# Four graph layers on one core: list keys and layer 0's row operations on other engines, and PSUM banks shared out anew

## The chip, the cores and the metric

The kernel runs on one core of one Trainium2 chip. The metric is the device time of one execution in microseconds (us); the time of the kernel before is the median of three runs. A core has five engines, which run side by side, each through its own list of instructions in a fixed order: TensorE (PE, matrix products), VectorE (DVE), ScalarE (ACT), GpSimd (POOL) and SyncE (SP, which issues most DMA transfers). An engine that has to wait holds up everything that stands behind in its list. SBUF is the on-chip memory that all of them use, and PSUM, eight banks of 128 x 512 numbers of 32 bits, is where TensorE writes. VectorE and ScalarE also read and write PSUM. GpSimd does not.

## The reference, cut to what matters

Eight batches of 2048 nodes with 64 features pass through four graph layers with one adjacency matrix. The matrix is sparse (some rows have over a hundred neighbours, most have a few), and each layer takes a softmax over a node's neighbours.

```python
# layer 0
h = jnp.maximum(_layernorm(x), 0.0)
x = x + attention(h, h, mask=adj)            # scores h.h / 8, values h
# layer 1
h = jnp.maximum(_layernorm(x), 0.0) @ W1
x = x + elu(softmax(leaky(h@a1 [:,None] + h@a2 [None,:]), adj) @ h)
# layer 2: four heads of dot-product attention with W_h, then W_o, one more attention, layer norm
# layer 3: as layer 1 with relu for elu
```

## The kernel before, in words

All eight batches are processed together: a row tile is 128 nodes by 512 numbers (8 batches x 64 features), and there are 16 row tiles, called i. A table in DRAM holds one row of 512 or 520 numbers for every node. A node's neighbours are fetched from it by indirect DMA, issued by GpSimd, one slot of 128 rows at a time (`gather`, L253). Each tile has a number of slots K for its nodes' first neighbours (`ROWS`, L29) and T packed slots for the neighbours left over (`PACKED`, L30). There are 81 slots in all. They land in a ring of 26 slots (`RING`, L33), so 26 gathers can be under way before the first slot has to be free again.

`edge_stack` (L62) writes the whole program. Inside, `pipeline` (L219) lays stages over the 16 tiles: in turn n, the last stage treats the oldest tile and the first stage the newest. A scheduler then arranges each engine's instructions. Within each layer the stages overlap, but between layers nothing does: a layer's gathers need every row of the table that the layer before wrote, the row of means among them (the neighbour of a node without any).

Five stretches follow each other.

- Stretch A (L711) normalises the 16 input tiles into table 0: row sums on VectorE (`norm_a`, L277), eight squares with a bias on ScalarE (L291), the sum of squares (L297), and eight scalings with relu on ScalarE (L308). `store_rows` (L362) stores the tile and adds it into `acc` on GpSimd (L367, L369). At the last tile, one product with `ones` makes the mean row (L372).
- Layer 0 (L712) builds each tile's neighbour lists and uses them. `load_adj` (L618) loads 128 x 2048 integers. `lists` (L622) turns each positive entry into a key, its column number counted from the right, in one VectorE operation (L627). VectorE's `max` then takes the eight largest keys of each segment (L633, `segments` L48, `SEGS` L32), with `match_replace` where more are wanted (L635), and again over the segments' results (L643, L645); small operations make the indices (L653, L708), masks (L655, L709) and selection matrices (L680). `take0` gathers; `first0` computes scores on VectorE (L432 to L441); `second` (L471) weights the gathered rows on GpSimd (L390) and sums them on TensorE (L395). `third0` (L483) divides on VectorE (L481), adds to x (L489), and normalises again (`norm_a` with `centre`: mean L281, subtraction L284, both on VectorE). `pre_c` scales on ScalarE, and table 1 is stored.
- Layer 1 (`additive`, L516) takes its scores from two numbers for each node, weights its rows on VectorE (L390 again), and projects on TensorE (L571). `products` (L331) prepares layer 2.
- Layer 2 (L725 to L860), the longest, weights on GpSimd and scores on VectorE.
- Layer 3 comes in two parts: the second attention of the reference's layer 2 (L863 to L912, weights on GpSimd) and the last additive layer (L920, weights on VectorE).

A helper called `tiny` (L231) hands out columns of one PSUM bank, as a place for small operands that VectorE then reads from PSUM: the mean in `norm_a` (L280), the node's own numbers and the weights in `additive` (L541, L556), and the squared norms in `first3` (L880). The bank is the only one in pool `ps_t`. The other pools in layers 0, 1 and 3 are `ps_q` with 3 banks, and `ps_m` and `ps_y` with 2 banks each.

The constants and weights are loaded at the very start (L143 to L205), ahead of the first input tile on SP.

## Time and profile before

| | us |
|---|---|
| median of 3 runs | 1628.55 (1625.19 to 1629.81) |
| the profiled execution | 1627.04 |
| its span, first to last instruction | 1625.3 |
| VectorE busy | 1289.1 (79%) |
| TensorE busy | 1209.7 (74%) |
| GpSimd busy | 1015.0 (62%) |
| ScalarE busy | 771.0 (47%) |

A group of instructions stands in the profile as its line, engine, operation, output<-inputs, shapes and count, then its busy time and the mean length of one in ns, and then how long the engine had idled before it and what ended that. The stretches can be told by their gathers: the first gather of layer 0 is issued at about 108 us, that of layer 1 at 399, of layer 2 at 610, of layer 3's first part at 1175 and of its second part at 1462. An engine's busy time over the whole span says little here, since each stretch has its own limit; the busy times by stretch are read in the prediction.

### The profile page before, as it was taken

The numbers are of one execution on the slowest core, as the hardware profiler recorded it, in microseconds if no ns is written. First come the engines' busy times: TensorE is split into PE (matmuls) and PEld (weight loads), VectorE is DVE, ScalarE is ACT, GpSimd is POOL, SyncE is SP. The second block draws the span as 40 slices with busy tenths as digits, with TensorE's granted clock in tenths as the row PEclk, the third lists the DMA queues.
The fourth block names the chain that finished last, engine by engine and source line by source line (L and its number), as shares of the span: only waits on it lengthen the run. The fifth ranks groups of instructions, "written<-read, shape, count | busy, mean of one in ns | idle before, by whom it ended". The sixth has DMA issues, their size and how long they took to land. (4 is left out here: it accounts for less than half of the span.)

```text
span 1625.3 us, 15664 instructions
## 1 busy us (share of the span) xinstructions
PE 1209.7 (74%) x3771; PEld 607.8 (37%) x3771; DVE 1289.1 (79%) x2594; ACT 771.0 (47%) x2522; POOL 1015.0 (62%) x823
## 2 busy tenths in 40 slices
PE   0024766876799983699987999999766878855997
PEld 0012243444454531234343344443333334423555
DVE  6978999994689996899999699871159979954677
ACT  5861323444377882456532455555426446760011
POOL 4345865664763006898689889898276686527550
PEclk9999787787899997799999999999967987857899
DMA  5545555453787448566265344400084453227771
GB/s 177 179 152 190 179 189 174 142 186 122 225 289 264 155 160 309 203 207 211 66 223 185 121 151 170 164 13 7 30 313 139 125 168 120 79 79 218 214 211 61
DMA packets 85786, 266.93 MB, mean 164 GB/s; under 512 B 14627, under 2 KB 14659, under 8 KB 75446
## 3 DMA queue, kind: packets, MB, share of 16 engines
q0 software_dynamic: 37328, 141.05, 28.0%
q1 hardware_dynamic: 48358, 124.79, 21.8%
q8 instruction: 32, 0.52, 0.1%
q14 instruction: 68, 0.56, 0.1%
HBM read 208.74 MB, written 57.05 MB: 164 GB/s over the span
## 5 line engine op out<-in xcount | busy, mean ns | idle before, releaser
L260 POOL DMA_INDIRECT g<-table,idx x405 | 396.3, 978 | 234.2 <-issue 135.2
L783 POOL TENSOR_TENSOR wh<-g,w 128x1024 f32<-128x1024 f32 x162 | 307.3, 1918 | 35.6 <-PE y L798 33.6
L395 PE MATMUL y<-wg,ident 128*128 128x512 f32 x392 | 240.9, 744 | 50.2 <-POOL wg L390 44.2
L390 POOL TENSOR_TENSOR wg<-g,w 128x1024 f32<-128x1024 f32 (+1 forms) x91 | 155.1, 1717 | 74.8 <-ACT w L446 44.6
L770 DVE TENSOR_REDUCE s<-prod 128x32 f32<-128x2048 f32 x81 | 183.8, 2285 | 20.3 <-ACT w L772 19.9
L798 PE MATMUL y<-wh,ident 128*128 128x512 f32 x320 | 155.7, 614 | 22.7 <-POOL wh L796 20.6
L395 PE MATMUL y<-wg,selt 128*128 128x512 f32 x256 | 138.6, 651 | 8.7 <-POOL wg L390 8.1
L395 PEld LDWEIGHTS y<-wg,ident 128*128 128x128 f32 x392 | 83.2, 232 | 136.3 <-issue 67.4
L798 PE MATMUL y<-wh,selt 128*128 128x512 f32 x256 | 125.1, 614 | 12.1 <-POOL wh L783 12.1
L806 ACT ACTIVATE yn<-y,rec 128x64 f32<-128x64 f32 x512 | 111.3, 367 | 30.4 <-PE y L798 29.7
L369 POOL TENSOR_TENSOR acc<-acc,xh 128x512 f32<-128x512 f32 x45 | 58.0, 1288 | 96.8 <-ACT xh L308 84.6
L766 DVE TENSOR_TENSOR prod<-q,g 128x2048 f32<-128x2048 f32 x49 | 111.4, 2274 | 3.6 <-ACT g L764 3.3
L390 DVE TENSOR_TENSOR wg<-g,tiny 128x1024 f32<-128x1024 f32 (+1 forms) x92 | 98.2, 1085 | 11.6 <-PE y L395 11.2
L452 DVE SCALAR_TENSOR_TENSOR zt<-m,bhc,att 128x512 f32<-128x512 f32 x64 | 47.1, 736 | 75.3 <-ACT att L451 75.3
L438 PE MATMUL q<-rows,sel 128*128 128x512 f32 x128 | 84.3, 762 | 17.6 <-DVE prod L440 9.2
L798 PEld LDWEIGHTS y<-wh,ident 128*128 128x128 f32 x320 | 59.6, 195 | 96.9 <-issue 62.6
L409 PEld LDWEIGHTS m<-w,selt 128*128 128x128 f32 x384 | 62.6, 211 | 88.4 <-issue 26.2
L308 ACT ACTIVATE xh<-x,ln_r 128x64 f32<-128x64 f32 x256 | 88.3, 428 | 14.6 <-POOL ln_r L302 13.6
L409 PE MATMUL m<-w,selt 128*128 128x8 f32 (+1 forms) x384 | 59.7, 258 | 44.9 <-ACT w L555 17.2
L764 ACT COPY g<-g 128x512 f32<-128x512 f32 x81 | 50.4, 622 | 86.5 <-DVE prod L766 77.4
L790 PE MATMUL y<-rows,ident 128*128 128x512 f32 x128 | 70.2, 634 | 18.7 <-DVE prod L766 13.6
L766 DVE TENSOR_TENSOR prod<-qe,g 128x2048 f32<-128x2048 f32 x32 | 72.9, 2279 | 12.9 <-DMA qe<-qtab,qidx 11.7
(208 smaller groups left out, 2515.9 us busy)
## 6 DMA issues: line engine op xcount, KB each, us to landing
qtab<-q SPq DMA_DIRECT2D x16, 1040.0 KB, 4.3
a<-in_adj_dram SPq DMA_DIRECT2D x16, 1024.0 KB, 7.0
q<-qtab SPq DMA_DIRECT2D x14, 1040.0 KB, 6.3
table<-xh SPq DMA_DIRECT2D x48, 256.0 KB, 2.2
rows<-table SPq DMA_DIRECT2D x48, 256.0 KB, 3.6
xs<-x SPq DMA_DIRECT2D x48, 256.0 KB, 2.4
x<-xs SPq DMA_DIRECT2D x48, 256.0 KB, 4.6
table<-xh SPq DMA_DIRECT2D x32, 260.0 KB, 2.0
```

Source lines behind the costliest of these rows:

```text
L260: g = nc.gpsimd.indirect_dma_start(out=ring[:, (held[i] + t) % RING, :cols], out_offset=None, in_=table[k][:, :], in_offset=bass.IndirectO ...
L308: nc.scalar.activation(dst[:, b * D:(b + 1) * D], st["src"][:, b * D:(b + 1) * D], func, bias=0.0 if st["less"] is None else r[:, 1, b:b + ...
L390: eng.tensor_tensor(wg[:, :m].rearrange("p t (b d) -> p t b d", b=B), g[:, :, :F].rearrange("p t (b d) -> p t b d", b=B), w[:, t0:t0 + m, ...
L395: nc.tensor.matmul(y, lhs(i, t), wg[:, t - t0, :], start=(t == 0 and own is None), stop=(t == n - 1))
L409: nc.tensor.matmul(p[:, :cols], selt(i, t), packed[:, t, :], start=(t == 0), stop=(t == T - 1))
L438: nc.tensor.matmul(qe, sel(i, t - K), q, start=True, stop=True)
L766: nc.vector.tensor_tensor(pr.rearrange("p (b h) d -> p b h d", h=H), q[:, :B * H * D].rearrange("p (b h d) -> p b h d", h=H, d=D), heads(g ...
L770: nc.vector.tensor_reduce(s[:, t - lo, :], pr, AX.X, OP.add)
L783: nc.gpsimd.tensor_tensor(wg, heads(row(i, t))[:, :, None, :].to_broadcast([P, B, 2, D]), w[:, :, 2 * k:2 * k + 2, None].to_broadcast([P, ...
L790: nc.tensor.matmul(st["ys"][j], ident, xb[:, 4 * j:4 * j + 4], start=True, stop=False)
L798: nc.tensor.matmul(st["ys"][j], lhs(i, t), wg[:, 4 * j:4 * j + 4], start=False, stop=(t == n - 1))
L806: nc.scalar.activation(yn[:, b, h, :], st["ys"][j][:, b, h, :], AF.Copy, scale=st["rec"][:, 4 * j + b, 2 * k + h:2 * k + h + 1])
```

## The change

The change has four parts.

1. *List keys on TensorE.* `load_adj` loads the adjacency in halves, and ScalarE takes the sign into a bf16 tile `e`. For each 512 columns, two bf16 products write the key into a PSUM bank of a new pool `ps_k`: 4096 times the entry plus the column's number. The searches read PSUM; one operation takes 4096 off again. Segments are cut at every 512 columns. The list stages come first in each turn and run further ahead of the rest (`ahead`, `lag`).
2. *Layer 0's row operations off VectorE.* In stretch A and layer 0 the mean and the subtraction run on GpSimd; in stretch A one VectorE operation replaces eight ScalarE scalings; `third0` divides on ScalarE and adds on GpSimd.
3. *The mean row* is summed by four small products for each tile and a VectorE addition, in place of GpSimd's `acc` addition, wherever a table has a mean row (tables 0, 1 and 4). The weights are loaded with the fourth list tile (`weights_in`).
4. *No `tiny` bank.* Its operands now lie in SBUF and its copies are gone; in layers 1 and 3 `ps_q` has 4 banks; in layer 0 `ps_q` and `ps_k` have 2 each.

```diff
+LIFT = 4096.0
...
+WAT = 3
+AHEAD0, LAG0 = (1, 0), [0, 1, 4, 5, 6, 7, 8, 9, 10]
...
+    marks = [n * k * k // (count * count) for k in range(1, count + 1)]
+    for at in range(512, n, 512):
+        near = min(range(count), key=lambda k: abs(marks[k] - at))
+        marks[near] = at
...
-    acc = const.tile([P, F], F32, name="acc")
+    acc = const.tile([P, F // P], F32, name="acc")
...
+    def weights_in(pool):
+        for t, w in ((wd1, w1), (wd3, w3)):
+            nc.gpsimd.memset(t, 0.0)
+            nc.sync.dma_start(out=t[:D, :D], in_=w)
+            nc.sync.dma_start(out=t[D:, D:], in_=w)
+        for u, wt, a in ((u1, w1t, a1), (u3, w3t, a3)):
...
-    def pipeline(*stages):
+    def pipeline(*stages, ahead=(), lag=None):
         states = {}
-        for n in range(NT + len(stages) - 1):
-            for s in reversed(range(len(stages))):
-                if 0 <= n - s < NT:
-                    i = order[n - s]
+        lag = lag or list(range(len(stages)))
+        turns = [s for s in ahead] + [s for s in reversed(range(len(stages))) if s not in ahead]
+        for n in range(NT + max(lag)):
+            for s in turns:
+                if 0 <= n - lag[s] < NT:
+                    i = order[n - lag[s]]
                     stages[s](i, states.setdefault(i, {}))
...
-    def tiny(n):
-        at = spot[0] if spot[0] + n <= F else 0
-        spot[0] = at + n
-        return bank[0][:, at:at + n]
...
-    def norm_a(src, st, centre):
+    def norm_a(src, st, centre, eng=nc.vector):
         s = small.tile([P, B], F32, name="ln_s")
         nc.vector.tensor_reduce(s, heads(src), AX.X, OP.add)
         st["sq"] = rows_pool[0].tile([P, F], F32, name="ln_sq", bufs=4)
         if centre:
-            mean = tiny(B)
-            nc.vector.tensor_scalar(mean, s, INV_D, None, op0=OP.mult)
+            mean = small.tile([P, B], F32, name="ln_m")
+            eng.tensor_scalar(mean, s, INV_D, None, op0=OP.mult)
             st["less"] = None
             st["src"] = rows_pool[0].tile([P, F], F32, name="ln_xc", bufs=3)
-            nc.vector.tensor_tensor(heads(st["src"]), heads(src), wide(mean), op=OP.subtract)
+            eng.tensor_tensor(heads(st["src"]), heads(src), wide(mean), op=OP.subtract)
             nc.scalar.activation(st["sq"], st["src"], AF.Square)
...
-    def pre_c(u):
+    def pre_c(u, eng=None):
         def f(i, st):
             st["xh"] = rows_pool[0].tile([P, F + B], F32, name="xh", bufs=3)
-            scaled(st["xh"], st, AF.Relu)
+            if eng is None:
+                scaled(st["xh"], st, AF.Relu)
+            else:
+                eng.scalar_tensor_tensor(heads(st["xh"][:, :F]), heads(st["src"]), 0.0,
+                                         wide(st["rstd"][:, 0, :]), op0=OP.max, op1=OP.mult)
...
         if mean:
+            C = F // P
+            p = ps_m.tile([P, F], F32, name="m")
+            for c in range(C):
+                nc.tensor.matmul(p[:, c:c + 1], xh[:, c * P:(c + 1) * P], ones, start=True, stop=True)
             if i == order[0]:
-                nc.gpsimd.tensor_copy(acc, xh[:, :F])
+                nc.vector.tensor_copy(acc, p[:, :C])
             else:
-                nc.gpsimd.tensor_tensor(acc, acc, xh[:, :F], op=OP.add)
+                nc.vector.tensor_tensor(acc, p[:, :C], acc, op=OP.add)
             if i == order[-1]:
                 p = ps_m.tile([P, F], F32, name="m")
-                nc.tensor.matmul(p[:1, :], ones, acc, start=True, stop=True)
-                mr = rows_pool[0].tile([1, F + B], F32, name="mr", bufs=1)
-                nc.vector.memset(mr[:, F:], 0.0)
-                nc.vector.tensor_copy(mr[:, :F], p[:1, :])
-                nc.sync.dma_start(out=table[k][N:N + 1, :], in_=mr[:, :cols])
+                nc.tensor.transpose(p[:C, :P], acc, ident)
+                mr = rows_pool[0].tile([C, P], F32, name="mr", bufs=1)
+                nc.vector.tensor_copy(mr, p[:C, :P])
+                nc.sync.dma_start(out=table[k][N, :F].rearrange("(c p) -> c p", p=P), in_=mr)
...
-    def second(i, st, wp=None, rec=None):
+    def second(i, st, eng=nc.gpsimd, rec=None):
...
-        st["y"] = weigh_sum(i, st, w) if wp is None else weigh_sum(i, st, wp, eng=nc.vector)
+        st["y"] = weigh_sum(i, st, w, eng=eng)
...
     def third0(i, st):
-        divide(st, st["y"])
-        add_store(i, st, st["y"], True)
-    def add_store(i, st, p, centre, more=0.0):
+        y = rows_pool[0].tile([P, F], F32, name="att")
+        for b in range(B):
+            nc.scalar.activation(y[:, b * D:(b + 1) * D], st["y"][:, b * D:(b + 1) * D], AF.Copy,
+                                 scale=st["rec"][:, b:b + 1])
+        x = st["x"]
+        nc.gpsimd.tensor_tensor(x, x, y, op=OP.add)
+        nc.sync.dma_start(out=xs[i], in_=x)
+        norm_a(x, st, True, nc.gpsimd)
+    def add_store(i, st, p, centre, more=0.0, eng=nc.vector):
         x = st["x"]
         nc.vector.scalar_tensor_tensor(x, p, more, x, op0=OP.add, op1=OP.add)
         nc.sync.dma_start(out=xs[i], in_=x)
-        norm_a(x, st, centre)
+        norm_a(x, st, centre, eng)
...
-            pr = tiny(2 * B)
-            nc.vector.tensor_copy(pr[:, :n], fs)
             pv = by_edge(i, fs, n)
             for t, m, g in rows(i, 0, K):
-                nc.vector.tensor_tensor(s[:, t:t + m, :], g[:, :, F:], pr[:, None, :B].to_broadcast([P, m, B]),
+                nc.vector.tensor_tensor(s[:, t:t + m, :], g[:, :, F:], fs[:, None, :B].to_broadcast([P, m, B]),
                                         op=OP.add)
...
             if k == 4:
-                nc.vector.tensor_tensor(s[:, :K, :], s[:, :K, :], pr[:, None, B:].to_broadcast([P, K, B]),
+                nc.vector.tensor_tensor(s[:, :K, :], s[:, :K, :], fs[:, None, B:].to_broadcast([P, K, B]),
                                         op=OP.subtract)
...
             nc.scalar.activation(w, s, AF.Exp)
-            wp = tiny((K + T) * B)
-            nc.vector.tensor_copy(wp, w.rearrange("p t b -> p (t b)"))
-            st["wp"] = wp.rearrange("p (t b) -> p t b", b=B)
         def check(i, st):
-            second(i, st, st["wp"], seen[:, i, :] if k == 1 else None)
+            second(i, st, nc.vector, seen[:, i, :] if k == 1 else None)
...
-                tc.tile_pool(name="ps_q", bufs=3, space=bass.MemoryType.PSUM) as ps_q, \
-                tc.tile_pool(name="ps_t", bufs=1, space=bass.MemoryType.PSUM) as ps_t:
-            bank[0] = ps_t.tile([P, F], F32, name="tiny")
-            keyrow = pool.tile([P, N], U16, name="keyrow", bufs=1)
-            nc.gpsimd.iota(keyrow, pattern=[[-1, N]], base=N + 1, channel_multiplier=0,
+                tc.tile_pool(name="ps_q", bufs=2, space=bass.MemoryType.PSUM) as ps_q, \
+                tc.tile_pool(name="ps_k", bufs=2, space=bass.MemoryType.PSUM) as ps_k:
+            keys = pool.tile([33, N], BF16, name="keys", bufs=1)
+            nc.gpsimd.memset(keys, 0.0)
+            nc.gpsimd.iota(keys[0:1, :], pattern=[[-64, N // 64], [0, 64]], base=N, channel_multiplier=0,
                            allow_small_or_imprecise_dtypes=True)
+            nc.gpsimd.iota(keys[32:33, :], pattern=[[0, N // 64], [-1, 64]], base=1, channel_multiplier=0,
+                           allow_small_or_imprecise_dtypes=True)
+            every = pool.tile([33, P], BF16, name="every", bufs=1)
+            nc.gpsimd.memset(every, 1.0)
+            lift = pool.tile([P, P], BF16, name="lift", bufs=1)
+            nc.scalar.activation(lift, ident, AF.Copy, scale=LIFT)
...
             def load_adj(i, st):
-                st["a"] = pool.tile([P, N], I32, name="a")
-                nc.sync.dma_start(out=st["a"], in_=adj[i * P:(i + 1) * P, :])
+                if i == order[WAT]:
+                    weights_in(pool)
+                st["e"] = pool.tile([P, N], BF16, name="e")
+                for c in range(0, N, N // 2):
+                    a = pool.tile([P, N // 2], I32, name="a")
+                    nc.sync.dma_start(out=a, in_=adj[i * P:(i + 1) * P, c:c + N // 2])
+                    nc.scalar.activation(st["e"][:, c:c + N // 2], a, AF.Sign)
             def lists(i, st):
                 K, T, W = ROWS[i], PACKED[i], WIDTH[i]
                 E = T * P
-                key = st["a"].bitcast(F32)
-                nc.vector.scalar_tensor_tensor(key, st["a"], 0.0, keyrow, op0=OP.is_gt, op1=OP.mult)
                 count, rounds = SEGS[i]
                 segs = segments(N, count, 8 * rounds)
                 c1 = pool.tile([P, len(segs), rounds, 8], F32, name=f"c{i}" if i < 2 else "c", bufs=1)
-                for s, (lo, hi) in enumerate(segs):
-                    for r in range(rounds):
-                        nc.vector.max(out=c1[:, s, r, :], in_=key[:, lo:hi])
-                        if r < rounds - 1:
-                            nc.vector.match_replace(out=key[:, lo:hi], in_to_replace=c1[:, s, r, :],
-                                                    in_values=key[:, lo:hi], imm_value=0.0)
+                for c in range(0, N, F):
+                    key = ps_k.tile([P, F], F32, name="k")
+                    nc.tensor.matmul(key, lift, st["e"][:, c:c + F], start=True, stop=False)
+                    nc.tensor.matmul(key, every, keys[:, c:c + F], start=False, stop=True)
+                    for s, (lo, hi) in enumerate(segs):
+                        if not c <= lo < c + F:
+                            continue
+                        lo, hi = lo - c, hi - c
+                        for r in range(rounds):
+                            nc.vector.max(out=c1[:, s, r, :], in_=key[:, lo:hi])
+                            if r < rounds - 1:
+                                nc.vector.match_replace(out=key[:, lo:hi], in_to_replace=c1[:, s, r, :],
+                                                        in_values=key[:, lo:hi], imm_value=0.0)
+                ends = c1.rearrange("p s r k -> p (s r k)")
+                nc.vector.tensor_scalar(ends, ends, LIFT, 0.0, op0=OP.subtract, op1=OP.max)
...
-            pipeline(xin_rows, lambda i, st: norm_a(st["x"], st, False), pre_b, pre_c(None), pre_d(0, None))
+            pipeline(xin_rows, lambda i, st: norm_a(st["x"], st, True, nc.gpsimd), pre_b,
+                     pre_c(None, nc.vector), pre_d(0, None))
             pipeline(load_adj, lists, take0, both(first0, xin_rows), second, third0, pre_b, pre_c(u1),
-                     pre_d(1, u1))
+                     pre_d(1, u1), ahead=AHEAD0, lag=LAG0)
...
-        with tc.tile_pool(name="more", bufs=1) as more_pool[0], psum_pools()[0] as ps_q, psum_pools()[1] as ps_t:
-            bank[0] = ps_t.tile([P, F], F32, name="tiny")
+        with tc.tile_pool(name="more", bufs=1) as more_pool[0], \
+                tc.tile_pool(name="ps_q", bufs=4, space=bass.MemoryType.PSUM) as ps_q:
...
-    with psum_pools()[0] as ps_q, psum_pools()[1] as ps_t, tc.tile_pool(name="rows2", bufs=2) as rp:
+    with tc.tile_pool(name="ps_q", bufs=4, space=bass.MemoryType.PSUM) as ps_q, \
+            tc.tile_pool(name="rows2", bufs=2) as rp:
         rows_pool[0] = rp
         order[:] = ORDER
-        bank[0] = ps_t.tile([P, F], F32, name="tiny")
...
-            pc = tiny(B)
-            nc.vector.tensor_copy(pc, c)
             s, w = scores(i, st, st["rows"]), slots(w_all, i)
             pv = by_edge(i, c, B)
-            nc.vector.tensor_tensor(s[:, :K], s[:, :K], pc[:, None, :].to_broadcast([P, K, B]), op=OP.subtract)
+            nc.vector.tensor_tensor(s[:, :K], s[:, :K], c[:, None, :].to_broadcast([P, K, B]), op=OP.subtract)
```

## The prediction

> **What bounds the kernel now.** I read first the busy times by stretch, since the stretches do not overlap. Columns: the stretch, its length, then busy time and count of PE, PEld (TensorE's weight loads), DVE, ACT and POOL, the granted clock, the DMA share, GB/s.
>
> ```profile
> 0.00:105.00 105.00, 3.92 (x13) 3.00 (x14) 78.77 (x258) 80.19 (x296) 40.59 (x67) 1.00 0.52 166
> 105.00:399.00 294.00, 202.21 (x616) 109.26 (x614) 263.02 (x811) 107.33 (x380) 184.25 (x142) 0.83 0.52 171
> 399.00:610.00 211.00, 178.84 (x651) 97.25 (x652) 173.49 (x339) 142.29 (x414) 80.21 (x96) 0.93 0.65 216
> 610.00:1175.00 565.00, 487.30 (x1366) 209.71 (x1365) 436.44 (x384) 270.56 (x852) 458.60 (x294) 0.96 0.43 147
> 1175.00:1462.00 287.00, 205.98 (x580) 106.36 (x580) 235.87 (x461) 154.43 (x529) 174.55 (x143) 0.77 0.45 146
> 1462.00:1626.00 164.00, 131.46 (x547) 82.24 (x547) 101.49 (x342) 16.20 (x51) 76.80 (x81) 0.86 0.59 174
> ```
>
> Stretch A, which ends near 105 us, has ScalarE and VectorE equally busy, on parts of a time of which the first 16.7 us go by before any input tile lands. In layer 0 VectorE is busy 263 of 294 us and every other engine has slack: the stretch is VectorE's. Layer 3's first part is VectorE's too (236 of 287). The last stretch is bound by none: in the chain of waits from 1470 to 1563 us gathers and their landings alternate with short work, and after that TensorE leads.
>
> Next, the groups of instructions before 400 us which the change touches (busy us, mean ns):
>
> ```profile
> L369 POOL TENSOR_TENSOR acc<-acc,xh 128x512 f32<-128x512 f32 x30 | 38.9, 1298 | 51.0 <-ACT xh L308 42.4 <-ACT xh L358 2.7 <-DVE c L645 1.6
> L627 DVE SCALAR_TENSOR_TENSOR a<-a,keyrow 128x2048 f32<-128x2048 int32 x16 | 38.2, 2390 | 7.7 <-DMA a<-in_adj_dram 7.7
> L481 DVE TENSOR_TENSOR y<-y,rec 128x512 f32<-128x512 f32 x16 | 11.0, 689 | 0.5 <-PE y L395 0.5
> L489 DVE SCALAR_TENSOR_TENSOR x<-y,x 128x512 f32<-128x512 f32 x16 | 10.9, 681 | 0.1
> L284 DVE TENSOR_TENSOR ln_xc<-x,tiny 128x512 f32<-128x512 f32 x16 | 10.8, 676 | 0.1
> L655 DVE TENSOR_SCALAR mba<-ell 128x2 f32<-128x2 f32 x6 | 6.3, 1053 | 0.0
> L655 DVE TENSOR_SCALAR mba<-ell 128x1 f32<-128x1 f32 x5 | 0.7, 142 | 0.0
> ```
>
> The last two rows are one operation on 2 and on 1 elements, 1053 against 142 ns. The timeline says why some operations of VectorE and GpSimd are so much longer than others:
>
> ```profile
> 122.00 2.29 DVE L627 SCALAR_TENSOR_TENSOR a<-a,keyrow 128x2048 f32<-128x2048 int32 x1 [0.47 <-DMA a<-in_adj_dram]
> 122.14 2.98 POOL L260 DMA_INDIRECT g<-table,idx  x1 [0.30 <-issue]
> ...
> 142.33 1.90 POOL L390 TENSOR_TENSOR wg<-g,w 128x1024 f32<-128x1024 f32 x1 [0.79 <-ACT ell L652]
> 143.15 3.23 DVE L627 SCALAR_TENSOR_TENSOR a<-a,keyrow 128x2048 f32<-128x2048 int32 x1
> 144.50 2.73 POOL L260 DMA_INDIRECT g<-table,idx  x1 [0.27 <-POOL wg L390]
> ```
>
> A gather alone takes 0.95 us; begun under L627, which reads two SBUF operands, it ends 0.83 us after L627. L627, begun under a GpSimd product, waits for that product's end. Each shuts the other out.
>
> **What the skill says.** The Trainium skill, *SBUF — State Buffer*, section "Who interferes with whom", names the cause: VectorE and GpSimd share a port pair under an exclusive lock, taken by VectorE's copies and scalar operations from SBUF to SBUF, and by its operations with two SBUF inputs against a GpSimd operation that reads SBUF. An operand in PSUM avoids that. The trace agrees (above), except on one inference there: it supposes that a two-input operation leaves descriptor generation alone, and here a gather went from 0.95 to 2.98 us. *VectorE: DVE Perf Modes*, "The perf-mode tier table", gives float32 two-input operations the same rate from SBUF and PSUM. In the timeline 512 elements follow each other every 0.60 us and 2048 every 2.20 with either source: 62 ns and 1.04 ns an element. *GPSIMD Engine Reference*, "Engine selection", calls GpSimd about half as fast on two inputs; the trace has 1.26 us (L369 undisturbed) against 0.60.
>
> **Part 1 and 2, stretch A and layer 0.** VectorE's sum, at those spacings: L627 goes, -16 x 2.20 = -35.3; in `third0` the division, addition, subtraction and mean go, -16 x (0.60 + 0.60 + 0.60 + 0.07) = -29.8; in stretch A one 0.60 scaling comes for a 0.07 mean, +8.4; taking off 4096 adds 14 x 0.13 + 0.20 + 0.43 = +2.4; the additions of column sums +2.2, less 1 for mean-row copies. Searches keep their element counts. Sum -53 us of VectorE's 342 (79 + 263).
>
> GpSimd, layer 0: 30 `acc` operations go from both stretches; each tile gains an addition, a subtraction (1.26 each) and a mean (0.25, from L302's smallest rows of 0.2): +44 in layer 0. Its load becomes 81 gathers x 1.25 (their spacing in the timeline) = 101, 78 of L390, and 44: 223 us. ScalarE loses L291 and L308 of stretch A (76 of its 80 busy us), and gains 16 squares (10), 32 signs (1.09 us each, an estimate from 0.27 us at 128 and 0.62 at 512 elements) and 128 divisions (28 us, by L806's 111.3 us for 512): slightly less in all. TensorE gains 128 bf16 products, no row of which exists; the skill's *TensorE: Matmul & The Clock Gate*, "Back-to-back issue gap", prices 512 columns at 216 ns at full clock and 427 at half, so 28 to 55 us, of which the latter half falls in layer 0. I take 35; with 202 busy there is room at a clock of 0.83.
>
> Now the path. SP issues the input tiles first, so they land at about 3.6 us (0.8 for the first issue, 2.8 to land as before) instead of 16.7. In the built order ScalarE does six signs ahead of its first square, and these follow half-tile loads through two buffers, so the first square is near 22 us (before 18.2). From there VectorE's order holds 36 us of work up to the mean row, at nearly full occupation 40: table 0 is ready at 66 us (before 105). GpSimd then has 26 gathers in front of its first product, the last eight of which need the packed list of tile 0, 44 us further down VectorE's list: 113 with a few waits, and 8 x 1.25 puts the first product at 123 (before 133.7). Behind it stand 55 gathers, 78 us of products and the 44, 190 us, against 160 on VectorE with some 17 us of lock waits (what the long rows of L653, L655, L708 and L709 add up to before). So GpSimd now sets the pace. At 87% occupation, between layer 2's 81% and the 87 to 90% of its best stretches, 190 becomes 218: the last subtraction ends at 341, before at 386. **-45 us**, and the 14 us tail to layer 1's first gather stays.
>
> **Part 3.** GpSimd loses 20 us in layer 3's first part. TensorE's four products a tile pipeline (L355 shows eight in 0.89 us): 7 us per table, hidden on an engine 72% busy. `acc` stood in the chain of waits there twice (1.28 each), so I count -4.
>
> **Part 4.** Removed: copies of 0.07 and 0.10 us a tile in layer 1 and the last layer, -2.7 each. The fourth `ps_q` bank frees TensorE from waits on VectorE (10.3 us for L339 in layer 1), but where these fall VectorE is 95% busy: nothing. Added is the lock.
> - Layer 3, first part: mean and subtraction (32 each) now read and write SBUF only. In the trace 12 of 32 means begin inside a GpSimd product, 11.8 us before its end in sum; a subtraction mostly comes behind its mean, when the way is free, so 9.6 more is the upper end. I take 14: with -4 this is **+10**.
> - Layer 1 and the last: 46 products each of up to 1.13 us now lock gathers out. 42 and 34 gathers overlap such a product before; if each had to wait for its end, 43 us each. Below is 0, if the ring's waits swallow it. Layer 1's second half has VectorE full and gathers ahead: +3, less copies, **0**. The last stretch waits for gathers up to 1563: the first 26 gathers run without a gap, and meet some six products: +8, less copies, **+5**.
> - Layer 2 is not touched and its order is nearly the old one: 0.
>
> Sum: -45 + 10 + 0 + 5 = -30. Against the profiled execution's 1627 (its span is 1625.3), that is 1597; the median of the runs stands 1.5 above it, inside their spread of 4.6. I forecast 1598.
>
> **Rivals.**
> - *GpSimd binds harder.* At 80% occupation (every gather waits for the ring, every product for an activation) layer 0 ends 19 us later: 1616. For it: GpSimd's list is in fixed order and takes three new steps a tile, each waiting for another engine. Against: five gathers which L627 stretched by about 2 us shrink again.
> - *Layer 0 gains more, locks less.* At 92%, 207 us for 190, and half the lock cost: 1578. For it: VectorE has 13 us more at the start. Against: GpSimd has never kept such a rate.
> - *The lock takes it all back, slower than before.* Places: gathers under L390's VectorE form, and layer 3's normalisation. Price: 43 + 42.5 + 21.4 = 107 us at most; from 45 us on the kernel is slower; at 60 it is 1642. For it: five of five gathers under L627 were stretched. Against: GpSimd is idle over half of both additive stretches.
> - That the keys cost as much in waits as they save: VectorE's searches would stand behind bank swaps of `ps_k`, 64 x up to 0.5 us = 32. It is inside the first rival's time.
>
> **Chances.** Forecast (1590 to 1612) 0.52; first rival 0.15; second 0.13; third 0.20. About 0.3% (5 us) is what a measurement can tell from no change. Of the first rival 0.03 and of the third 0.03 fall there: faster 0.77, same 0.06, slower 0.17. The range, 1574 to 1636, leaves out the far halves of the second and third.
>
> **What would show it.** First layer-0 gather near 68 us, first GpSimd product near 123, layer 1's first gather near 355; GpSimd the busiest engine of layer 0. VectorE's L390 rows unchanged, with gathers of over 1.5 us beneath them; means of over 0.5 us in layer 3. Wrong if table 0 is later than 85 us, if layer 0 stays over 280 us long, or if the additive stretches grow by over 15 us each.

## The result, and the profile after

The changed kernel takes 1609.0 us (median of four runs, 1607.3 to 1616.0) where the kernel before takes 1626.9 in the same rounds. The ratio is 0.9893, with a 95% interval of 0.986 to 0.9925: about 18 us faster. I had forecast 1598, 30 us faster than the profiled run before. The profiled run of the changed kernel is the longest of its four, 1616.0 us with a span of 1614.2, so the two profiles differ by only 11 us, and some 7 us of what differs by stretch below may be chance of this one execution.

The busy times by stretch, now cut at the changed kernel's own first gathers. The columns are those of the prediction: stretch, length, then busy time and count of PE, PEld, DVE, ACT and POOL, granted clock, DMA share, GB/s.

```profile
0.00:77.00 77.00, 45.74 (x163) 31.57 (x163) 52.00 (x193) 29.39 (x68) 37.56 (x72) 1.00 0.76 229
77.00:367.00 290.00, 236.50 (x848) 131.88 (x847) 242.47 (x836) 151.05 (x530) 195.05 (x174) 0.86 0.54 173
367.00:591.00 224.00, 186.62 (x665) 100.96 (x666) 176.00 (x314) 147.19 (x427) 90.20 (x97) 0.91 0.63 210
591.00:1151.00 560.00, 477.73 (x1353) 207.68 (x1351) 431.04 (x378) 264.61 (x839) 458.15 (x293) 0.96 0.43 146
1151.00:1446.00 295.00, 221.82 (x707) 123.71 (x707) 247.38 (x460) 153.57 (x529) 158.91 (x128) 0.76 0.44 142
1446.00:1614.00 168.00, 133.93 (x547) 81.92 (x547) 96.88 (x310) 16.77 (x51) 84.84 (x81) 0.86 0.57 170
```

Measured from the first gather of a layer to that of the next, the stretches compare as follows. In the profile before, the first gather of layer 0 stands at 109.5 us and that of layer 2 at 615.9, not near 105 and 610, where the prediction cut, so the 211 us that it gives layer 1 are 216 here.

| stretch | before | after | difference | forecast |
|---|---|---|---|---|
| A | 109.5 | 77.5 | -32.0 | together |
| layer 0 | 290.5 | 289.5 | -1.0 | -45 |
| layer 1 | 216.0 | 224.5 | +8.5 | 0 |
| layer 2 | 560.5 | 559.9 | -0.6 | 0 |
| layer 3, first part | 287.0 | 294.2 | +7.2 | +10 |
| last stretch | 161.9 | 168.6 | +6.7 | +5 |

The gain lies in stretch A and layer 0, as forecast, but is 12 us smaller there. Parts of it are given back in layer 1, in layer 3 and in the last stretch. VectorE's busy time in A and layer 0 went from 342 to 294 us (forecast: 53 less, found: 47 less).

Three things are seen in single rows. First, the waits of VectorE up to 77 us and those of GpSimd in layer 0 (columns: engine, line, what released it, then total, number, longest in us):

```profile
DVE bhl L191 <- DMA bhc<-in_bh_dram: 12.9, 1, 12.9
...
POOL g L244 <- DVE mbb L677: 27.3, 1, 27.3
```

The first is a wait that I had not looked for: L191, which scales two bias columns, was moved up to be eighth in VectorE's list as it ran, and stands there from 9.0 to 22.0 us for a small load. The second is the wait for tile 0's list, which I had seen in the order: GpSimd has 18 gathers behind it by 102 us and gets the next index at 129.6.

Second, three groups of the page after, and below them two of the page before (line, engine, operation, shapes and count, then busy us, mean ns, idle before):

```profile
L244 POOL DMA_INDIRECT g<-table,idx x405 | 404.5, 999 | 279.5 <-issue 122.4
L381 DVE TENSOR_TENSOR wg<-g,w 128x1024 f32<-128x1024 f32 (+1 forms) x92 | 99.2, 1090 | 13.9 <-PE y L386 13.1
L357 PE MATMUL m<-ones,xh 128*128 128x1 f32 x384 | 69.2, 303 | 10.5 <-DVE idx L714 3.8
```

```profile
L260 POOL DMA_INDIRECT g<-table,idx x405 | 396.3, 978 | 234.2 <-issue 135.2
L390 DVE TENSOR_TENSOR wg<-g,tiny 128x1024 f32<-128x1024 f32 (+1 forms) x92 | 98.2, 1085 | 11.6 <-PE y L395 11.2
```

The mean products (L357) keep TensorE busy for 69 us, 23 a table, where I had put 7. VectorE's products (L381) take what they took (1085 ns before). The mean gather rose from 978 to 999 ns although layer 0's gathers fell from 1068 to 962, so those of layer 1 and of the last stretch have become longer: 0.95 to 1.04 and 1.05 us. The timeline of layer 1 shows how (start, length, engine):

```profile
444.31 0.95 POOL L244 DMA_INDIRECT g<-table,idx  x1 [0.30 <-issue]
...
445.31 1.22 DVE L381 TENSOR_TENSOR wg<-g,w 128x1024 f32<-128x1024 f32 x1
445.56 1.79 POOL L244 DMA_INDIRECT g<-table,idx  x1 [0.30 <-DVE s L449]
...
447.65 0.94 POOL L244 DMA_INDIRECT g<-table,idx  x1 [0.30 <-issue]
```

The gather of 445.56 begins inside VectorE's product, which ends at 446.53, and itself ends at 447.35, 0.82 us later. In these two stretches 35 gathers begin inside such a product. 30 of them take over 1.0 us, and each of the 30 ends 0.81 to 0.85 us after its product; the other five begin in the product's last 0.12 us and take 0.94 to 0.95. (One more gather takes over 1.0 us, the first of layer 1 with 1.03, outside any product.) The 31 gathers that began outside a product and were still under way when one began took 0.94 to 0.97 us, as if alone. Before, 48 gathers began inside a product, 44 of them more than 0.12 us before its end; the weights then came from PSUM, and not one took over 0.98 us. The excess is 6.9 us in layer 1 and 8.5 in the last stretch.

Third, layer 3's first part on VectorE, after and before:

```profile
L268 DVE TENSOR_TENSOR ln_xc<-z,ln_m 128x512 f32<-128x512 f32 x16 | 14.0, 874 | 0.3 <-ACT xh L292 0.3
L268 DVE TENSOR_TENSOR ln_xc<-x,ln_m 128x512 f32<-128x512 f32 x16 | 12.0, 753 | 0.1
L265 DVE TENSOR_SCALAR ln_m<-ln_s 128x8 f32<-128x8 f32 x32 | 9.6, 312 | 0.1
```

```profile
L284 DVE TENSOR_TENSOR ln_xc<-z,tiny 128x512 f32<-128x512 f32 x16 | 10.8, 673 | 0.1
L284 DVE TENSOR_TENSOR ln_xc<-x,tiny 128x512 f32<-128x512 f32 x16 | 10.9, 681 | 0.2
L281 DVE TENSOR_SCALAR tiny<-ln_s 128x8 f32<-128x8 f32 x32 | 5.1, 160 | 0.2
```

The sums of single durations rose by 4.4 us (subtractions), 4.9 (means) and, which I had not priced, 4.3 for the subtraction of the squared norms (L889, longest 3.12). That is 9.3 us for the two operations for which I had taken 14, and 13.6 in all.

### The profile page after: what moved, and what is told of

Same layout as the page of the kernel before. It is cut to its first block, busy times and chain, and to the rows that moved or that the text cites. A ratio compares the mean times of both kernels' runs of the same rounds, so it can differ in the third digit from the quotient of the medians.

```text
span 1614.2 us, 16603 instructions
## 1 busy us (share of the span) xinstructions
PE 1302.3 (81%) x4280; PEld 677.7 (42%) x4280; DVE 1245.8 (77%) x2489; ACT 762.6 (47%) x2443; POOL 1024.7 (63%) x844
## 5 line engine op out<-in xcount | busy, mean ns | idle before, releaser
L244 POOL DMA_INDIRECT g<-table,idx x405 | 404.5, 999 | 279.5 <-issue 122.4
L386 PE MATMUL y<-wg,ident 128*128 128x512 f32 x392 | 227.7, 708 | 21.1 <-POOL wg L381 13.1
L381 POOL TENSOR_TENSOR wg<-g,w 128x1024 f32<-128x1024 f32 (+1 forms) x91 | 156.6, 1735 | 83.8 <-ACT w L437 54.4
L386 PE MATMUL y<-wg,selt 128*128 128x512 f32 x256 | 144.7, 674 | 3.0 <-DVE wg L381 1.8
L386 PEld LDWEIGHTS y<-wg,ident 128*128 128x128 f32 x392 | 79.9, 223 | 105.8 <-issue 63.8
L381 DVE TENSOR_TENSOR wg<-g,w 128x1024 f32<-128x1024 f32 (+1 forms) x92 | 99.2, 1090 | 13.9 <-PE y L386 13.1
L400 PE MATMUL m<-w,selt 128*128 128x8 f32 (+1 forms) x384 | 60.5, 258 | 48.5 <-ACT w L550 21.1
L429 PE MATMUL q<-rows,sel 128*128 128x512 f32 x128 | 78.7, 720 | 15.8 <-ACT w L437 6.8
L301 ACT COPY xt<-q 128x512 f32<-128x512 f32 x80 | 45.8, 582 | 67.8 <-PE q L300 67.4
L357 PE MATMUL m<-ones,xh 128*128 128x1 f32 x384 | 69.2, 303 | 10.5 <-DVE idx L714 3.8
```

The costliest lines, as they stand in the source:

```text
L244: g = nc.gpsimd.indirect_dma_start(out=ring[:, (held[i] + t) % RING, :cols], out_offset=None, in_=table[k][:, :], in_offset=bass.IndirectO ...
L357: nc.tensor.matmul(p[:, c:c + 1], xh[:, c * P:(c + 1) * P], ones, start=True, stop=True)
L381: eng.tensor_tensor(wg[:, :m].rearrange("p t (b d) -> p t b d", b=B), g[:, :, :F].rearrange("p t (b d) -> p t b d", b=B), w[:, t0:t0 + m, ...
L386: nc.tensor.matmul(y, lhs(i, t), wg[:, t - t0, :], start=(t == 0 and own is None), stop=(t == n - 1))
L400: nc.tensor.matmul(p[:, :cols], selt(i, t), packed[:, t, :], start=(t == 0), stop=(t == T - 1))
L429: nc.tensor.matmul(qe, sel(i, t - K), q, start=True, stop=True)
```

## The experiments

The twelve runs come in three groups of four, each on its own chip (numbers 1, 15 and 6). On all three the kernel before takes 1675 to 1677 us (medians 1675.5, 1675.4, 1676.6), 3% more than beside the pair above, whose chip is not on record. I call the three "the other chips"; that the pair ran on another one, and not on one of them at another time, is an inference. The granted clock is not the difference: it is 0.891 in the first profile, and 0.891 and 0.892 in those of tiny_back and keys_only, at 1640 and 1670 us. Each time is compared only with others of these chips, by its ratio to the kernel before in the same group. What differs there is the subject of the third group. Lines in the variants are those of the changed kernel, shifted by a few.

| run | median us | ratio to before | 95% interval |
|---|---|---|---|
| keys_only (part 1, weights loaded late) | 1675.7 | 0.9997 | 0.9977 to 1.0017 |
| tiny_acc (parts 1, 2, weights loaded late) | 1666.5 | 0.9942 | 0.9915 to 0.9969 |
| tiny_back (parts 1 to 3) | 1644.1 | 0.9825 | 0.979 to 0.986 |
| banks3 (parts 1 to 3, no small bank) | 1648.2 | 0.984 | 0.9813 to 0.9867 |
| after_again (all) | 1635.3 | 0.977 | 0.9741 to 0.9798 |
| after_third (all) | 1639.8 | 0.9786 | 0.9752 to 0.982 |
| bias_late | 1632.0 | 0.975 | 0.9724 to 0.9775 |
| later0 | 1650.9 | 0.9842 | 0.9809 to 0.9876 |
| all_three | 1654.9 | 0.989 | 0.9851 to 0.9929 |
| spare_bank | 1667.3 | 0.9941 | 0.992 to 0.9962 |
| spare_bank_bl | 1661.8 | 0.9924 | 0.9897 to 0.995 |

And the stretches of the profiled executions, in us. Two executions of one kernel, after_again and after_third, differ by up to 4.8 us in a stretch:

| run | A | layer 0 | layer 1 | layer 2 | layer 3 first | last |
|---|---|---|---|---|---|---|
| before_again | 110.1 | 288.1 | 237.2 | 559.4 | 294.1 | 184.1 |
| keys_only | 110.8 | 291.1 | 237.1 | 561.8 | 291.7 | 175.9 |
| tiny_acc | 87.3 | 306.4 | 239.4 | 559.8 | 292.5 | 181.2 |
| tiny_back | 78.5 | 292.5 | 237.4 | 559.8 | 291.3 | 178.4 |
| banks3 | 76.6 | 290.9 | 242.1 | 561.9 | 295.7 | 175.9 |
| after_again | 80.1 | 290.7 | 233.2 | 558.6 | 294.2 | 177.5 |
| after_third | 78.1 | 290.8 | 231.9 | 561.3 | 299.0 | 177.0 |
| bias_late | 75.2 | 288.6 | 232.8 | 558.7 | 295.5 | 179.3 |
| later0 | 77.5 | 307.6 | 234.3 | 560.1 | 294.4 | 177.5 |
| all_three | 73.4 | 306.9 | 239.9 | 561.6 | 290.6 | 178.5 |
| spare_bank | 77.6 | 291.1 | 239.0 | 560.7 | 300.0 | 197.1 |
| spare_bank_bl | 76.6 | 288.6 | 236.0 | 560.1 | 300.1 | 193.1 |

### First group: the change taken apart

*tiny_back* puts the small bank back in layers 1 and 3, with its copies and with 3 `ps_q` banks:

```diff
-            mean = small.tile([P, B], F32, name="ln_m")
+            mean = tiny(B) if bank[0] is not None else small.tile([P, B], F32, name="ln_m")
...
+            wp = tiny((K + T) * B)
+            nc.vector.tensor_copy(wp, w.rearrange("p t b -> p (t b)"))
...
-                tc.tile_pool(name="ps_q", bufs=4, space=bass.MemoryType.PSUM) as ps_q:
+                tc.tile_pool(name="ps_q", bufs=3, space=bass.MemoryType.PSUM) as ps_q, \
+                tc.tile_pool(name="ps_t", bufs=1, space=bass.MemoryType.PSUM) as ps_t:
```

> The changed kernel with the small PSUM bank back in layers 1 and 3 (mean of the normalisation, the node's own numbers, the weights, the squared norms; copies as before) and 3 ps_q banks there. Theory (the port lock): no gather of layer 1 and the last stretch is over 1.05 us any more, layer 1 goes from 224 back to 211-213, the last stretch from 169 to 162-164, layer 3's first part from 294 to 287 or less, layer 2 loses its 5: about -22, 1587 us. Rival (the fourth ps_q bank reorders TensorE's work in layer 1, and the lock costs little): the same gain, but then the run with 3 banks and no small bank has it too. Rival (the stretches differ by chance between single executions): within 4 us of the changed kernel's 1609.

*banks3* changes only the count of `ps_q` banks, from 4 to 3, in layers 1 and 3.

> The changed kernel with 3 ps_q banks in layers 1 and 3 and still no small bank. Theory (the port lock): gathers are stretched as in the changed kernel (a dozen over 1.2 us in layer 1 and in the last stretch each), the time is within 4 us of 1609. Rival (order by the fourth bank): layer 1 falls from 224 to about 211 and the time to about 1596.

Between these two runs only the small bank and its copies differ, so they price the lock (less the copies): 1644.1 against 1648.2 us, with intervals that overlap. The longest gather of layer 1 and the last stretch is 1.03 us with the bank; without it 12 and 16 of them are over 1.2. Layer 1 is 4.7 us shorter with the bank, layer 3's first part 4.4, layer 2 2.1; the last stretch is 2.5 longer. The lock shows in every trace with these operands in SBUF, but its price on these chips is a few us at most, hardly clear of the noise, and not the 22 expected. The prices of the other half of part 4 follow below, when the changed kernel stands beside them.

*tiny_acc* takes tiny_back and sums the mean row on GpSimd again (the weights are still loaded where part 3 put them):

```diff
-                nc.tensor.matmul(p[:, c:c + 1], xh[:, c * P:(c + 1) * P], ones, start=True, stop=True)
...
-                nc.vector.tensor_tensor(acc, p[:, :C], acc, op=OP.add)
+                nc.gpsimd.tensor_tensor(acc, acc, xh[:, :F], op=OP.add)
```

> As the run with the small bank back, and the mean row is summed on GpSimd again (part 3 undone in all three tables). Theory of the prediction (GpSimd sets the pace of layer 0, four mean products a tile are hidden): layer 0 gets 20 us of GpSimd's at 87% occupation, +23, layer 3's first part +4, stretch A 0 to +10: 27 to 37 us slower than the run with the small bank. Rival (TensorE, 88% busy in layer 0 with 36 us of mean products, and 45 us of them in stretch A, sets the pace too): layer 0 shrinks by 10 to 20, stretch A by about 3, the run is 10 to 20 us faster. If both engines bind about equally: within 8 us.

It is 22.4 us slower than tiny_back. The busy times of stretch A and layer 0, first of tiny_back, then of tiny_acc:

```profile
0.00:78.50 78.50, 46.23 (x164) 31.75 (x165) 53.29 (x195) 29.88 (x68) 37.67 (x72) 1.00 0.72 224
78.50:371.00 292.50, 238.62 (x847) 132.81 (x846) 241.25 (x835) 150.45 (x530) 195.00 (x174) 0.86 0.53 171
```

```profile
0.00:87.30 87.30, 23.15 (x45) 5.31 (x45) 65.30 (x208) 31.42 (x71) 58.37 (x89) 1.00 0.68 213
87.30:393.70 306.40, 223.32 (x711) 110.06 (x711) 234.44 (x790) 148.31 (x526) 214.34 (x191) 0.88 0.50 160
```

GpSimd gets 20 us more in each and the stretches grow by 8.8 and 13.9; TensorE loses 23 and 15. 12.7 of the 13.9 us come behind GpSimd's first product, where its busy time is 17.5 us more. So GpSimd's work does lengthen layer 0 behind that product, and the relief of TensorE, 82% busy in tiny_back's layer 0, doesn't make up for it. Whether VectorE, 82% busy too, holds the stretch beside GpSimd no run tells. The growth is less than the 23 us forecast for layer 0.

*keys_only* takes tiny_acc and puts the row operations back as well (`third0` on VectorE, stretch A's scalings on ScalarE), so that of the four parts nearly part 1 alone is left. Two things of the others stay: the weights are loaded with the fourth list tile, which is tile 0, and `ps_q` has two banks in layer 0.

> Part 1 alone: list keys on TensorE, with the small bank in layers 1 and 3, the mean row on GpSimd, and layer 0's row operations on VectorE and ScalarE as before. Theory (VectorE's sum counts): VectorE loses 31 us net by the keys; stretch A stays about 105 us long, since ScalarE has 80 us of squares and scalings and 11 of signs there; layer 0 falls from 290 to about 270: 1600 to 1606 us. Rival (the keys give back in waits for their two PSUM banks what they save): 1617 to 1627.

It gains nothing: 0.9997. VectorE's busy time in A and layer 0 falls to 318 us, from 339 in before_again, yet layer 1 begins at 402 us, against 398. Its stretch A and layer 0:

```profile
0.00:110.80 110.80, 23.16 (x45) 5.31 (x45) 67.17 (x254) 92.76 (x312) 38.38 (x72) 1.00 0.53 168
110.80:402.00 291.20, 225.21 (x712) 112.13 (x711) 250.66 (x809) 126.03 (x397) 176.53 (x143) 0.85 0.53 169
```

Stretch A is held by ScalarE (93 of 111 us; 81 of 110 in before_again), and VectorE idles 44 us of it. In layer 0 the list of tile 0 ends later: the first GpSimd product comes at 164.9 us, in before_again at 134.1. From there the run catches up. Counted from the layer's first gather it is 30 us behind before_again at GpSimd's first product, 16 at the tenth, and level at the fortieth of 45 (247.5 and 247.7 us). About 12 us of the late start are waits in which VectorE stands between 120 and 134 us, at a copy of the moved weights (L174) and in the lists:

```profile
DVE u L174 <- issue: 6.4, 1, 6.4
DVE mbb L718 <- remote: 2.5, 1, 2.5
...
DVE st L669 <- issue: 1.9, 1, 1.9
...
DVE eq L711 <- issue: 1.2, 1, 1.2
```

"issue" and "remote" mean that the profile finds no instruction that ended the wait. Neither of my two explanations is what the run shows. VectorE's saved time is not eaten by bank waits (VectorE waits 4.0 us for `ps_k` banks in stretch A, 2.0 in layer 0). In stretch A it is idle, since ScalarE has that stretch; in layer 0 a late start takes back what is caught up behind it, and that start is in part the moved weights'. What part 1 is worth without them was not measured.

Read downwards, the table of times gives each part's worth on top of those before it: part 1, with the weights moved, nothing; part 2 9 us; the rest of part 3 22 us; part 4 4 to 9 us, at the edge of what the intervals tell. No run leaves out part 1 and keeps the others.

### Second group: stretch A and the wait for tile 0

*after_again* is the unaltered kernel.

> The changed kernel, unaltered, beside its variants. If the port lock is what layer 1 lost, its layer 1 and last stretch hold a dozen gathers of over 1.2 us each, and the run stands 11 to 22 us above the one with the small bank back and within 4 us of the one with 3 ps_q banks and no small bank. If the fourth bank is what hurts, it stands 5 us or more above the latter. If the fourth bank helps, it stands 5 us or more below the latter.

The gathers are stretched as expected (9 and 16 over 1.2 us). But the run stands 9 us below tiny_back, not above it, and 13 below banks3, both of the first group: of the three cases laid down, the last. On these chips, by the medians, the fourth bank gains more than the lock costs. Layer 1 is where: 233 us against 242 with three banks.

*bias_late* moves the scaling of the bias columns:

```diff
-        nc.vector.tensor_scalar(bhl, bhc, SLOPE, None, op0=OP.mult)
...
+            low = nc.vector.tensor_scalar(bhl, bhc, SLOPE, None, op0=OP.mult)
+            tc.add_manual_dep(low.ins, taken[1, order[0]].ins.name, mybir.DependencyInfo(
+                mybir.DependencyClass.Sync, mybir.DependencyReason.DATA), reason="low")
             bounds(0, seen, 0)
```

> The changed kernel with one instruction of VectorE moved: the scaling of the bias columns (128x2) stands at the end of layer 1 and no longer sixth in VectorE's list. Theory: its wait for the bias load (12.9 us, until 22.0) holds up the first keys (ready at 17) and the fifth row sum, and is 5 of the 11 us by which stretch A missed its forecast: table 0 is ready 4 to 7 us earlier, and so is the end. Rival: from 28 us on stretch A is paced by VectorE's order and the three ln_xc buffers, and GpSimd is busy until 16.9 anyway: at most 2 us.

Stretch A is 75.2 us long, 2.9 and 4.9 less than in the two runs of the unaltered kernel; the median is 3.3 us lower than after_again's, with intervals of the ratio that overlap. VectorE's search starts at 18.3 instead of 23.7 us, but then another wait takes the place of the one removed:

```profile
DVE ln_s L260 <- POOL ln_m L264: 8.8, 1, 8.8
```

The fifth row sum needs a buffer that GpSimd's means still read, and GpSimd gets to them at 17 us, after its setup work. So the bias is some 3 to 5 of the 9.5 us by which the first gather missed its forecast (77.5 us for "near 68"), as far as single profiles tell; that lies between the 4 to 7 of my theory and the 2 of its rival.

*later0* makes tile 0 the sixth:

```diff
-MAKING = [15, 14, 13, 0, 12, 11, 10, 1, 9, 2, 8, 3, 7, 4, 6, 5]
+MAKING = [15, 14, 13, 12, 11, 0, 10, 1, 9, 2, 8, 3, 7, 4, 6, 5]
```

> The changed kernel with tile 0 made sixth and no longer fourth (its list keeps VectorE for 39 us while GpSimd waits 27 us for it). Theory: the mean row stands 7 us earlier in VectorE's list and the first product 30 us; the first GpSimd product falls from 139 to about 110, and since GpSimd sets the pace of layer 0 behind it, layer 0 ends 15 to 28 us earlier. Rival (VectorE's sum sets the end of layer 0, wherever GpSimd starts): 0 to 8 us earlier. Rival (tile 0's 17 slots in the middle of the 26-slot ring block the gathers behind): slower by 5 to 15.

It is 15.6 us slower than after_again. GpSimd's first product does come at 108.4 us, but its second tile begins only at 159.3. Between 109 and 161 us VectorE is at work on the list of tile 0, as its busy time shows (49.5 of 52 us):

```profile
109.00:161.00 52.00, 33.77 (x83) 12.11 (x82) 49.47 (x228) 18.18 (x36) 14.54 (x14) 0.67 0.55 182
```

and GpSimd, with gathers ahead of it, waits for scores that stand behind that list in VectorE's order:

```profile
POOL wg L381 <- issue: 29.7, 1, 29.7
```

The wait was moved, not removed. None of the three cases describes it; the third has the sign and, with up to 15 us, the size, but the ring isn't the cause.

*all_three* joins tiny_back, bias_late and later0.

> The small bank back in layers 1 and 3 with 3 ps_q banks, the bias scaling at the end of layer 1, and tile 0 made sixth. The three act in different stretches, so their gains should add: the sum of the gains of the three single runs within 6 us, 25 to 45 us below the changed kernel beside it. If a gain in layer 0 is only moved into the start of layer 1 or layer 2, less than two thirds of the sum.

It is 19.6 us slower than after_again. The single differences to after_again are +8.8 (tiny_back, from the first group), -3.3 and +15.6, in sum +21.1; the run agrees, and the expectation failed since two of the three gains weren't any.

### Third group: the other chips, and small operands in spare banks

*before_again* is the kernel before, for one profile.

> The kernel before, profiled beside the changed one on a chip where it takes about 1675 us. If the longer time there comes from slow landings of the gathers, the excess over its first profile sits in layer 1 and the last stretch (15 to 25 us each); stretch A and layer 0 stay at 110 and 290, layer 3's first part at 287 to 292. If everything is 3% slower there, each stretch is longer by 3%.

A, layer 0 and layer 2 are within 2.4 us of the first profile. Layer 1 is 21.2 us longer, the last stretch 22.2, layer 3's first part 7.1. In all three 26 gathers go out without a gap at the start (so they do in layer 2, which isn't longer), and there ScalarE and VectorE now stand still although their operands, by the recorded ends, are ready; the profile calls the release "remote". ScalarE's waits in layer 1, of before_again and then of after_again:

```profile
ACT e L580 <- remote: 28.1, 1, 28.1
```

```profile
ACT xt L301 <- remote: 14.1, 1, 14.1
ACT e L572 <- remote: 8.2, 1, 8.2
```

No wait of layers 1 and 3 in the first pair of profiles is put down to such a release. The traces tell two things more. In layers 1 and 3 of before_again and after_again each of these waits hangs on the semaphore, the signal, that TensorE's instructions raise, and it is raised 2 to 23 us after the last TensorE instruction recorded before it, 22.7 us for the wait of 28.1. So what is late there is TensorE, whose ends the profile models, or the word of it. And slow landings, which I had supposed, are not it: the packets of layer 1's first 26 gathers had all been moved 34.7 us after the first was issued, in the first profile 35.4; in the last stretch it was 34.5 and 34.9. What makes TensorE late wasn't found out. *after_third*, the unaltered kernel in this group, has its layer 1 and last stretch as expected, 231.9 and 177.0 us.

> The changed kernel, unaltered, as the anchor for the two below: layer 1 at 233 and the last stretch at 178 where the kernel before takes 1675 us, at 224 and 169 where it takes 1627.

*spare_bank* keeps four `ps_q` banks and puts the weights and the means (not the node's own numbers and the squared norms) into banks that are held anyway:

```diff
+        if eng is nc.vector:
+            wp = spare[0][:, F // 2:F // 2 + SLOTS[i] * B]
+            nc.vector.tensor_copy(wp, w.rearrange("p t b -> p (t b)"))
+            w = wp.rearrange("p (t b) -> p t b", b=B)
...
-            norm_a(t, st, True)
+            norm_a(t, st, True, spare=y[:, :B])
```

> The changed kernel with its four ps_q banks, but VectorE's small operands in PSUM again, in banks that are held anyway: the mean of layer 3 over the start of a bank just used up, the weights of layer 1 and the last stretch in the free half of the bank of the weights' sums (a copy of 0.2 us a tile). Theory (the lock costs, the fourth bank gains): no gather of layer 1 and the last stretch over 1.05 us, layer 3's first part 3 to 4 shorter, layer 1 4 to 8 shorter than the changed kernel's, the last stretch the same or 5 shorter: 6 to 16 us below the changed kernel beside it. Rival (stretched gathers cost nothing, since the ring's waits swallow them, and copies and longer-held banks cost): within 3 us, or slower by up to 6.

The lock is gone from the trace (no gather of layer 1 and the last stretch over 1.03 us), and the run is 27 us slower than after_third: 20 in the last stretch, 7 in layer 1. Both sides had it wrong. In the last stretch TensorE waits 28.0 us for ScalarE's copies (`xt`), 20.5 of them at once, and that copy waits 20.0 us for a "remote" release, again on TensorE's semaphore, raised 19.9 us after the last recorded instruction. Whether the banks, held until the last product, bring this about wasn't told apart.

*spare_bank_bl* adds bias_late to it.

> As the run with the spare banks, and the scaling of the bias columns at the end of layer 1 besides. The two lie in different stretches: 3 to 6 us below the run with the spare banks alone, by a stretch A of 75 us; if that gain was a chance of single executions, within 2 us of it.

5.5 us below spare_bank, by medians, but stretch A is only 1.0 us shorter in the profiles. No variant is shown to beat the changed kernel: bias_late's interval overlaps with that of both runs of the kernel unaltered.

## Why the prediction was right, and where it failed

**Direction and place: right.** The gain comes from stretch A and layer 0, through work taken off the engines that hold them; layer 3 and the last stretch give a little back.

**Stretch A: first gather at 77.5 us instead of near 68.** The step that failed is "at nearly full occupation 40: table 0 is ready at 66 us". The first square came at 27.9 us instead of 22, since the fifth row sum and the first searches stood behind L191, and ScalarE's signs ahead of the square waited for their loads. bias_late takes 3 to 5 us of it back, on another chip. From 28 us on VectorE was busy 44 of 49 us, so the rest is the sum itself, which was larger than the 36 us I had counted. VectorE's list I had added up, but not searched for waits on the weight loads, which part 3 moves.

**Layer 0: the length right, the reason in the main.** The first product came at 139 us instead of 123: 9.5 by the late table, the rest because tile 0's list was ready 52 us after the first gather instead of 45. From there to the end of GpSimd's list 216 us passed (forecast 218), with 171 us busy and 55 gathers at 0.3 us more of spacing, so 187 us or 87% occupied (forecast 190 and 87%). tiny_acc supports that GpSimd has the pace: 20 us more of it cost 13.9, and 15 us less of TensorE don't make up for them. Two of my own signs failed, though. "GpSimd the busiest engine of layer 0": VectorE was busy 242 us, TensorE 237, GpSimd 195; behind the first product TensorE was busy 189 of 216 us and VectorE 186, as much as GpSimd with its spacing, so the pace isn't shown to be GpSimd's alone. And "if layer 0 stays over 280 us long" would have called the prediction wrong: it stayed at 289.5. That sign contradicted my own sum, in which layer 0 runs from 68 to 355 us, 287 long. Two prices of TensorE's work were too low: the key products, taken for 35 us in layer 0, kept it busy for 42 (60 us in all, where 28 to 55 were priced), and the wrong price of the mean products (7 us a table, from eight records in 0.89 us; measured 23, as the mean of 285 ns in the same row of before, L355, would have told). Whether either cost time no run tells.

**What each part is worth: not seen.** I summed parts 1 and 2 on VectorE and took the removal of `acc` for 4 us and a term of GpSimd's sum. On the other chips part 1 with the moved weights is worth nothing, and the rest of part 3, on top of parts 1 and 2, 22 us. That VectorE's time comes to bear only when ScalarE no longer holds stretch A and GpSimd is relieved in layer 0 is an inference from the loads: no run leaves out part 1 alone. The whole came out with the sign and the places forecast, and 18 us for 30, since each step of the sum was made on the changed kernel's own engine loads.

**Layer 1: +8.5 instead of 0.** The failed step is "Layer 1's second half has VectorE full and gathers ahead: +3, less copies, 0". It is the first half that costs. In the last stretch I had counted the first 26 gathers, which run without a gap and meet VectorE's products (+8, less copies); layer 1 begins in the same way, and I left it out. This is read from the one pair of profiles. Up to the fourth addition to x, layer 1 is 7.6 us late (68.4 against 60.8 us after the layer's first gather); the distance is 13.0 us at the eighth and again 7.7 at the last. In its first 70 us, VectorE waits longer for gathers, before and after:

```profile
DVE s L545 <- DMA g<-table,idx: 12.1, 3, 7.2
```

```profile
DVE s L540 <- DMA g<-table,idx: 20.2, 8, 7.2
```

The upper end of the lock was also five to six times too high (43 us for each stretch, 6.9 and 8.5 found): I let every gather that overlaps a product wait for its end, and only those that begin inside one do. One sum on the lock doesn't follow from my own terms either: the third rival weighs it against 45 us alone, but layer 3's 4 us and the copies' 5.4 stand on the same side, so the kernel would have been slower from some 54 us of lock on, and 60 would have made it about 1633 us, not 1642.

**The fourth `ps_q` bank: not nothing.** I costed it at nothing because VectorE is full where TensorE waits for it. On the other chips four banks stand 8 to 13 us below three, 9 to 10 of them in layer 1. It offsets the lock there, so part 4 gained 4 to 9 us in the experiments by the medians, while in the first pair layer 1 and the last stretch got 15 us longer. On the other chips the standstills at the start of these two stretches leave time in which a late gather costs nothing; that this is why the first pair lost time there and these runs did not is an inference, since no variant ran beside the first pair.

**Layer 3 and the last stretch: right in the first pair,** +7.2 for +10 and +6.7 for +5. In layer 3 the means and subtractions got 9.3 us longer where I took 14, and 4.3 more fell in a subtraction that I had not named. The other chips don't confirm the two sums: against before_again, layer 3's first part is 0.1 and 4.9 us longer in the two profiles of the changed kernel, and the last stretch 6.6 and 7.1 shorter.

## What to carry to other kernels

Work taken off the busiest engine pays only in stretches which that engine holds, as stretch A of keys_only shows: name the holder of each stretch after the change, not before it. A part that gains nothing alone may still be needed beside others; to know, run the change without that part, which was not done here. When instructions move, read each engine's new list for waits on loads that have moved too, small ones above all: one scaling of 128x2 numbers held VectorE for 13 us. Where two engines lock each other out, count the instructions that *begin* under the other's, and look first at the bursts (a layer's first 26 gathers), where nothing else hides the delay.

## What the runs showed of the hardware

- A gather's issue is held by a two-input VectorE product from SBUF only if it begins inside it: of 35 such gathers the 30 that began more than 0.12 us before the product's end ended 0.81 to 0.85 us after it, all 31 that were under way when a product began took 0.94 to 0.97 us, and the products took 1090 ns on average, against 1085 before. (In after_again two gathers that began within 0.03 us of a product's start went free too.) The Trainium skill, *SBUF — State Buffer*, section "Who interferes with whom", infers that such an operation leaves descriptor generation alone; these traces show that it doesn't, at the gather's start. With the weights in PSUM none of 48 was held, as the section's rule on one SBUF input has it.
- One program can differ by 3% between sessions, and by place: the kernel before took 1627 us beside the first pair and 1675 on each of three chips, and the whole difference lies in three of the four stretches that begin with 26 gathers without a gap. There, TensorE's signal came up to 23 us after the last TensorE instruction on record. Layer 1 and the last stretch of the changed kernel were together 15 us longer than before in the first pair; on chips 15 and 6 both are shorter than in before_again.
